# Last image's 3x3 convolution: nine taps per 8 rows, against four products of combined rows per 16 rows

## The chip, the cores and the metric

The kernel runs on one core of a Trainium2 chip. The metric is the device time of one execution in microseconds (us). TensorE (PE) does matrix products, VectorE (DVE), ScalarE (ACT) and GpSimd (POOL) work on elements, and SyncE (SP) issues the transfers.

## The reference, cut to what matters

Four images of 64 x 64 pixels and 96 channels pass four layers: a state-space layer with scans along rows and columns (layer 0), a separable convolution (layer 1), attention and a feed-forward net (layer 2), a Fourier filter and a feed-forward net (layer 3). Layer 1 is what is changed:

```python
y = jax.nn.relu(x)
y = lax.conv_general_dilated(y, dw_kernel, padding='SAME', feature_group_count=C)   # 3x3, per channel
y = y + dw_bias
y = lax.conv_general_dilated(y, pw_kernel, padding='SAME')                          # 1x1, 96 -> 96
y = y + pw_bias
inv = gamma * lax.rsqrt(moving_var + BN_EPS)
y = y * inv + (beta - moving_mean * inv)
...
t = t + attention(layernorm(t)); t = t + ffn2(layernorm(t))
t = t + filter(layernorm(t));    t = t + ffn3(layernorm(t))
```

All data are float32, but for the feed-forward nets, whose operands are rounded to fp8.

## The kernel before, in words

Channels lie on partitions, the 4096 pixels of an image along the free dimension, in 8 blocks of 512 (`BLK`, `NBLK`), each 8 rows of 64 (`RPB`, `HW`).

There are three parts in time. First a head: image 0's inputs for the scans. Then a long middle in which the scans of all four images run, in an order written out by hand (`tc.manual_schedule()`), while a planner (`pieces`, with credits per engine) puts the later layers of images 0 to 2 beside them. At last an end: `last_post` finishes layer 0 of image 3 (into `x1t`, the tile `side`, which stays in on-chip memory), beside the last of image 2's feed-forward net, and then `tail` calls `rest` for image 3. Head and end are outside the hand-written order: there, instructions of several generators are emitted in turn, and the order on an engine need not be that of emission.

`rest` is a list of stages. In its first, `layer1` does the convolution for one image. The constants merge depthwise and pointwise weights: `taps[:, ky * 3 + kx, :]` is the 1x1 matrix `pw` scaled per input channel by the 3x3 weight of that tap, so that both convolutions are one sum of nine 96 x 96 products. For a block of 8 rows, nine matmuls (L953) add up in one bank of PSUM (`p_l1`; the profile calls it `p_l`), each with a shifted window of the input:

```python
nc.tensor.matmul(
    p3[:, ra:rb, ca_:cb_], lhsT=taps[:, ky * 3 + kx, :],
    rhs=x[:, at + ra : at + rb, ca_ + dx : cb_ + dx], start=(k == 0), stop=(k == 8))
```

A tap that looks left or right leaves out a column, so it has 504 columns in place of 512; at the image's top and bottom a row is left out too. One ACTIVATE on ScalarE (L925) applies `l1s` (the scale and bias of the normalisation) and writes the block into `t`. VectorE does nothing for it.

What follows needs `t`: `layernorm(..., "t1", "ln_a")` begins with its first half of four blocks when `ready["t1"]` is 4, and its second half at 8. It takes the mean away by a matmul (`p_mean`, L997), copies the result on VectorE (L988), squares it on ScalarE (L989), sums the squares up by matmuls (`p_var`, L979), and scales (`p_rstd` L1049, DVE L1040). Then come attention (`p_tok`, `p_gram`, `p_att`), the feed-forward net, the filter and the last net.

The end uses eight banks of PSUM in turn (`bank_taker`), the first of which image 2's feed-forward net had last.

Image 0's convolution of layer 0 has a form of the kind that the change brings in: `convolve_pairs` in the head combines rows on VectorE (L448), multiplies (L463), and adds up on ScalarE and VectorE (L477 to L484).

Of the kernel before, what the change touches and what calls it, by code (L numbers as in the profile page):

```python
# [10 lines left out]
F32 = mybir.dt.float32  # L11
F16 = mybir.dt.float16
F8 = mybir.dt.float8e5
AF = mybir.ActivationFunctionType
ALU = mybir.AluOpType
# [4 lines left out]
HW = 64  # L20
L = HW * HW
C = 96
# [4 lines left out]
BLK = 512  # L27
NBLK = L // BLK
RPB = BLK // HW
# [4 lines left out]
def conv_taps():  # L34

    return [(1, 1)] + [(y, x) for y in range(3) for x in range(3) if (y, x) != (1, 1)]


def tap_window(ky, kx, r0):

    dy, dx = ky - 1, kx - 1
    ra, rb = max(0, -dy - r0), min(RPB, HW - dy - r0)
    ca, cb = max(0, -dx), min(HW, HW - dx)
    return dy, dx, ra, rb, ca, cb
# [4 lines left out]
NEXT = "next"  # L49
# [24 lines left out]
def layers(ctx: ExitStack, tc: tile.TileContext, a: dict, out):  # L74
# [4 lines left out]
    nc = tc.nc  # L79
# [11 lines left out]
    def dram(name, shape):  # L91
        return [dr.tile(shape, F32, tag=f"{name}{b}", name=f"{name}{b}") for b in range(NB)]
# [9 lines left out]
    x1 = dram("x1", [C, L])  # L102
# [20 lines left out]
    def steps_past(since, n):  # L123

        while ordered[0] and clock[0] < since + n:
            yield NEXT
# [8 lines left out]
    done = {}  # L135
# [44 lines left out]
    def rows_of(i):  # L180

        r0 = RPB * i
        return r0, max(r0 - 1, 0), min(r0 + RPB + 1, HW)
# [5 lines left out]
    def bank_taker(pool, n):  # L189

        free = [(pool, k) for k in range(n)]

        def take(name, rows=C, cols=BLK, held=()):
            while not free:
                yield NEXT
                if held:
                    yield from settle(held)
            bank = free.pop(0)
            t = bank[0].tile([128, BLK], F32, tag=f"bank{bank[1]}", name=name)

            def give(later=False):

                if later and ordered[0]:
                    returned.append((free, bank))
                else:
                    free.append(bank)

            return t[:rows, :cols], give

        return take, free  # L210

    def settle(held):


        while held:
            cost, f, args, since = held[0]
            if cost[1]:
                while ordered[0] and clock[0] == since and (clock[0] - 1) % 8 in (7, 0, 1):
                    yield NEXT
            yield cost  # L220
            held.pop(0)
            f(*args)

    def until(ready):
        while not ready():
            yield NEXT
# [641 lines left out]
    def blk(i):  # L868
        return slice(i * BLK, (i + 1) * BLK)
# [25 lines left out]
    def rest(b, take, deep, x1t=None, held=None):  # L895
# [3 lines left out]
        t = outer.sbuf(f"t{b}").tile([C, L], F32, tag="t", name="t")  # L899
        ready = {}  # L900
# [4 lines left out]
        def layer1(wk):  # L905
            x3 = (x1[b] if x1t is None else x1t).rearrange("p (r w) -> p r w", w=HW)

            def load(i):
                r0, lo, hi = rows_of(i)
                if x1t is not None:  # L910
                    return x3[:, lo:hi, :], clock[0]
                x = wk.tile([C, RPB + 2, HW], F32, tag="x", name="x", bufs=2)
                nc.sync.dma_start(x[:, : hi - lo, :], x3[:, lo:hi, :])
                return x, clock[0]

            def arrived(i):
                return done.get(("x1", b), 0) >= min(i + 2, NBLK)

            yield from until(lambda: arrived(0))
            nxt = load(0)  # L920
            yield NEXT
            held = []

            def finish(i, p, give):
                nc.scalar.activation(  # L925
                    t[:, blk(i)], p, AF.Identity, scale=l1s[:, 0:1], bias=l1s[:, 1:2]
                )
                give()
                ready["t1"] = i + 1

            for i in range(NBLK):
                r0, lo, hi = rows_of(i)
                if nxt is None:
                    yield NEXT
                    yield from settle(held)
                    yield from until(lambda: arrived(i))
                    nxt = load(i)
                    yield NEXT
                (x, since), nxt = nxt, None
                if clock[0] < since + LANDING:  # L940
                    yield NEXT
                    yield from settle(held)
                    yield from steps_past(since, LANDING)
                p, give = yield from take("p_l1", C, held=held)
                p3 = p.rearrange("p (r w) -> p r w", w=HW)
                for k, (ky, kx) in enumerate(conv_taps()):
                    if k % 3 == 0:
                        yield (2.4, 0, 0, 0, 0 if k else 1)
                        if nxt is None and i + 1 < NBLK and arrived(i + 1):
                            nxt = load(i + 1)  # L950
                    dy, dx, ra, rb, ca_, cb_ = tap_window(ky, kx, r0)
                    at = r0 + dy - lo
                    nc.tensor.matmul(  # L953
                        p3[:, ra:rb, ca_:cb_], lhsT=taps[:, ky * 3 + kx, :],
                        rhs=x[:, at + ra : at + rb, ca_ + dx : cb_ + dx],
                        start=(k == 0), stop=(k == 8),
                    )
                    if k == 2:
                        yield from settle(held)
                held.append(((0, 0.68, 0, 0), finish, (i, p, give), clock[0]))  # L960
            yield NEXT
            yield from settle(held)

        def layernorm(wk, hold, dst, source, result, previous=None):


# [451 lines left out]
        wk = normal.sbuf(f"ln{b}")  # L1418
# [3 lines left out]
        if deep > 1:  # L1422
# [4 lines left out]
        wk = mid.sbuf(f"mid{b}")  # L1427
        q8 = wk.tile([C, L], F8, tag="q8", name="q8")
        yield [
            *layernorm(wk, ln[:C, :], ln[:C, :], "t3", "ln_s", "q8"),  # L1430
            *feed_forward(wk, ffn2, q8, "q8", "t3"),
            *layernorm(wk, ln[:C, :], q8, "t2", "q8"),
            attention(wk, ln),
            *layernorm(wk, ln[:C, :], ln[:C, :], "t1", "ln_a"),
            layer1(wk),
        ], [mid] + ([held] if held else [])
        inner = Region(tc)
        yield filter_in(inner.sbuf(f"filter_in{b}"), ln), [inner, normal]
# [3 lines left out]
        vs = wide.sbuf(f"vs{b}").tile([128, N1, C], F32, tag="vs", name="vs")  # L1442
# [9 lines left out]
        wk = last.sbuf(f"last{b}")  # L1452
# [10 lines left out]
    def main_lane(take):  # L1463

        region = Region(tc)
        wk = region.sbuf("pre")
        images = [before_scans(b, wk, take, prev=b - 1 if b > 1 else None) for b in range(1, NB)]
        yield [chain(*parts) for parts in zip(*images)], [region, weights]
        done["pre"] = True
        for b in range(NB - 1):  # L1470
            yield from rest(b, take, 1)
# [33 lines left out]
    def tail(x1t, held):  # L1505

        region = Region(tc)
        take, _ = bank_taker(region.psum("tail_psum"), 8)
        yield from rest(NB - 1, take, 2, x1t, held)
        region.close()  # L1510
# [12 lines left out]
    def place_of(n, q):  # L1523


        return (4, 3, 2, 1)[q] if n % 2 else q
# [3 lines left out]
    while len(delta_places) <= N:  # L1530
        p = delta_places[-1]
# [204 lines left out]
    aside, weights, head, start = Region(tc), Region(tc), Region(tc), Region(tc)  # L1736
# [3 lines left out]
    wk = weights.sbuf("weights", side="right")  # L1740
    kept.append(const("gavg", [C, C], a["gavg"], wk))
    take, _ = bank_taker(start.psum("start_psum"), 2)
# [43 lines left out]
    wk = head.sbuf("pre0")  # L1786
    take, _ = bank_taker(head.psum("head_psum"), 8)
# [9 lines left out]
    take, banks = bank_taker(beside.psum("beside_psum"), 3)  # L1797
# [3 lines left out]
    with tc.manual_schedule():  # L1801
        ordered[0] = True
        pas = [decay(0, 0, True), None, None, None]
        for n in range(N + 1):
# [3 lines left out]
            for q in range(NCH):  # L1808
# [23 lines left out]
                s = Ss[n, q] = big.tile([128, CH], F32, tag=f"S{place_of(n, q)}", name="S")  # L1832
# [14 lines left out]
            if n % NG == 1 and n > 1:  # L1847
                b, o = halves[h - 1]
# [53 lines left out]
            if n % NG == NG - 4 and h + 1 < len(halves):  # L1902
                b, o = halves[h + 1]
# [7 lines left out]
    x1t = side[:, :L]  # L1911
# [125 lines left out]
```

## Time and profile before

| | us |
|---|---|
| median of the runs (5784.04, 5797.89, 5817.91) | 5797.89 |
| profiled execution: its own time | 5791.5 |
| profiled execution: span from first to last instruction | 5789.7 |
| image 3's layer 1 in it, first to last matmul start | 5412.3 to 5479.1 |

The page gives busy time by engine over the whole span: PE 72%, DVE 84%, ACT 52%, POOL 76%, and a mean granted TensorE clock of 0.771 of full speed. These are means over parts with different limits; what bears on the change is the stretch from 5388 to 5500 us. A float32 matmul of the program stands as two records in the trace (144 for the 72 of one image); below, one record is called a pass. The duration of a pass includes its latency; the pace is the distance from one start to the next.

### The profile page before, as it was taken

How to read it: one execution, taken by the hardware profiler on the slowest of the kernel's cores; microseconds unless marked ns; L12 is line 12 of the kernel's file. 1: busy time of each engine (PE TensorE's matmuls, PEld its weight loads, DVE VectorE, ACT ScalarE, POOL GpSimd, SP SyncE). 2: the span in 40 equal slices, each digit the busy share in tenths (PEclk: the TensorE clock that was granted, in tenths of full speed). 3: DMA queues.
4: the chain of work that ended last, by engine and by line, in shares of the span. 5: the costliest groups of instructions: out<-in, count | busy, mean ns of one | idle time of the engine just before them, and what ended most of it. 6: DMA issues, size and time to landing. Idle time of an engine off the chain costs nothing. (4 is left out here: it accounts for less than half of the span.)

```text
span 5789.7 us, 65093 instructions
## 1 busy us (share of the span) xinstructions
PE 4187.2 (72%) x19818; PEld 1630.1 (28%) x19818; DVE 4858.5 (84%) x3610; ACT 3020.1 (52%) x4188; POOL 4417.0 (76%) x2148
## 2 busy tenths in 40 slices
PE   8978887778864777664477776667778667667878
PEld 4422222222211221241331221334222114323345
DVE  4188988888899898999799999999999999978364
ACT  4767766766663356545454446444544544434233
POOL 1378887888898778888788989888898898867200
PEclk9888898888866876666777886678678666777888
DMA  4378878876699878788988868679887678886013
GB/s 123 111 212 229 233 200 235 233 204 196 195 252 236 225 206 222 207 240 244 255 235 224 228 182 222 197 210 248 235 235 202 171 207 237 251 227 183 20 43 101
DMA packets 470107, 1174.80 MB, mean 203 GB/s; under 512 B 90768, under 2 KB 155900, under 8 KB 469628
## 3 DMA queue, kind: packets, MB, share of 16 engines
q1 hardware_dynamic: 469756, 1170.64, 74.1%
q8 instruction: 157, 2.57, 0.2%
q14 instruction: 194, 1.59, 0.1%
HBM read 1013.53 MB, written 156.76 MB: 202 GB/s over the span
## 5 line engine op out<-in xcount | busy, mean ns | idle before, releaser
L1574 POOL TENSOR_TENSOR S<-S,rep 128x1024 f32<-128x1024 f32 x768 | 1807.2, 2356 | 546.2 <-DVE S L1894 495.1
L1587 ACT ACTIVATE pa<-dl,nega 128x1024 f32<-128x1024 f32 x1152 | 1285.3, 1117 | 1431.9 <-DVE S L1894 1072.3
L1570 POOL TENSOR_TENSOR B<-B,rep 128x1024 f32<-128x1024 f32 x768 | 1798.0, 2355 | 119.0 <-DMA B<-du_s 70.8
L1833 DVE TENSOR_TENSOR_SCAN S<-pa,S,B 128x1024 f32<-128x1024 f32 x576 | 1352.3, 2348 | 315.6 <-ACT pa L1587 133.5
L1601 PE MATMUL py<-S,red 128*32 128x512 f32 x3072 | 908.5, 848 | 755.1 <-POOL S L1574 503.6
L1884 DVE TENSOR_TENSOR_SCAN pa<-pa,edge,B 128x1024 f32<-128x1024 f32 x438 | 1029.7, 2351 | 55.5 <-ACT pa L1587 55.5
L1894 DVE TENSOR_TENSOR S<-S,pa 128x1024 f32<-128x1024 f32 x630 | 763.6, 1212 | 1.9
L1833 DVE TENSOR_TENSOR_SCAN S<-pa,B 128x1024 f32<-128x1024 f32 x192 | 436.4, 2273 | 44.8 <-ACT pa L1587 35.8
L1601 PEld LDWEIGHTS py<-S,red 128*32 128x32 f32 x3072 | 110.0, 125 | 1232.7 <-POOL S L1574 728.3
L402 PE MATMUL p_conv<-low,conv_w 128*96 128x512 f32 x864 | 437.4, 658 | 14.1 <-ACT u L414 9.6
L1884 DVE TENSOR_TENSOR_SCAN pa<-pa,B 128x1024 f32<-128x1024 f32 x192 | 440.8, 2296 | 5.3
L154 ACT COPY side<-side 96x256 f32<-96x256 f32 (+1 forms) x448 | 279.0, 629 | 187.7 <-DMA deltaT_s<-side 79.9
L1884 DVE TENSOR_TENSOR_SCAN dl<-pa,edge,B 128x1024 f32<-128x1024 f32 x138 | 323.1, 2341 | 20.6 <-ACT pa L1587 16.6
L1175 POOL CAST h<-y 128x1536 fp8e5<-128x1536 f16 x64 | 95.5, 1492 | 303.2 <-ACT y L886 281.9
L1579 POOL TENSOR_TENSOR dl<-dl,rep 128x1024 f32<-128x1024 f32 x138 | 325.6, 2360 | 0.1
L402 PE MATMUL p_conv<-high,conv_w 64*96 64x512 f32 (+1 forms) x576 | 269.7, 605 | 0.0
L997 PE MATMUL p_mean<-t,centre 96*96 96x512 f32 x256 | 173.7, 791 | 99.0 <-ACT sq L989 48.4
L402 PEld LDWEIGHTS p_conv<-low,conv_w 128*96 128x96 f32 x864 | 149.5, 181 | 319.0 <-issue 289.8
L1601 PE MATMUL py<-dl,red 128*32 128x512 f32 x552 | 220.2, 717 | 21.1 <-POOL dl L1579 21.1
L1609 ACT COPY ys<-py 128x512 f32<-128x512 f32 x384 | 221.8, 578 | 19.5 <-PE py L1601 18.3
L647 PE MATMUL p_y<-side,ident 96*96 96x512 f32 x336 | 210.0, 774 | 28.1 <-DVE side L681 8.6
L953 PE MATMUL p_l<-x,taps 96*96 96x504 f32 (+3 forms) x432 | 199.4, 613 | 16.2 <-DMA x<-x 12.7
(245 smaller groups left out, 6024.0 us busy)
## 6 DMA issues: line engine op xcount, KB each, us to landing
dl<-delta_s SPq DMA_DIRECT2D x768, 256.0 KB
B<-du_s SPq DMA_DIRECT2D x768, 256.0 KB
B<-duT_s SPq DMA_DIRECT2D x768, 256.0 KB
dl<-deltaT_s SPq DMA_DIRECT2D x768, 256.0 KB
z_s<-z SPq DMA_DIRECT2D x48, 512.0 KB
zl<-z_s SPq DMA_DIRECT2D x64, 384.0 KB
side<-y_s SPq DMA_DIRECT2D x120, 192.0 KB
rep<-bc_s SPq DMA_DIRECT2D x64, 256.0 KB
```

Source lines behind the costliest of these rows:

```text
L154: nc.scalar.copy(o.rearrange("p (w h) -> p w h", h=HW), t[:n, :].rearrange("p (h w) -> p w h", w=HW)[:, q * w : (q + 1) * w, :],)
L402: nc.tensor.matmul(p, lhsT=conv_w[: src.shape[0], k, oc * C : (oc + 1) * C], rhs=src[:, ky : ky + RPB, kx : kx + HW], start=(k == 0), stop ...
L647: nc.tensor.matmul(p, lhsT=ident[:C, :C], rhs=x, start=(j == 0), stop=(j == 2))
L1570: nc.gpsimd.tensor_tensor(Bs[n, q], Bs[n, q], reps[n // NG, 0, q], ALU.mult)
L1574: nc.gpsimd.tensor_tensor(Ss[n, q], Ss[n, q], reps[n // NG, 1, q], ALU.mult)
L1579: nc.gpsimd.tensor_tensor(dls[n, 0], dls[n, 0], reps[n // NG, 1, 0], ALU.mult)
L1587: nc.scalar.activation(pa, dls[n, q], AF.Exp, scale=nega[:, g : g + 1])
L1601: nc.tensor.matmul(py[32 * j : 32 * j + 32, :], lhsT=red, rhs=x[:, k * BLK : (k + 1) * BLK], start=(i == 0), stop=(i == len(terms) - 1),)
L1609: nc.scalar.copy(ys, pys.pop((n, half)))
L1833: nc.vector.tensor_tensor_scan(s, pas[q], Bs[n, q], Ss[n, q - 1][:, CH - 1 : CH] if q else 0.0, ALU.mult, ALU.add,)
L1884: nc.vector.tensor_tensor_scan(to[:, ::-1], pas[q][:, ::-1], Bs[n, q][:, ::-1], edge if k else 0.0, ALU.mult, ALU.add,)
L1894: nc.vector.tensor_tensor(Ss[n, q], Ss[n, q], to, ALU.add)
```

## The change

For image 3 alone, `layer1` is replaced by `layer1_pairs`. It takes 16 rows at a time as 8 pairs of an even and an odd row. Of the three kernel rows g0, g1, g2 (each three taps) it makes four combinations once: g0, (g0 + g1 + g2) / 2, (g0 - g1 + g2) / 2, g2. For each group it makes four combinations of input rows on VectorE, v0 to v3, with columns of zeros at both sides (set once by GpSimd, for two sets of buffers), multiplies each by its combination with three shifts along the row, and forms even and odd output rows from the four products. That is 4 x 3 matmuls of 512 columns for 16 rows, where `layer1` has 2 x 9.

```diff
+        def layer1_pairs(wk):
+            x3 = x1t.rearrange("p (j r w) -> p j r w", r=2, w=HW)
+            g = [taps[:, 3 * k : 3 * k + 3, :] for k in range(3)]
+            two = wk.tile([C, 2, 3, C], F32, tag="two", name="two")
+            plus, minus = two[:, 0], two[:, 1]
+            nc.vector.tensor_tensor(plus, g[0], g[2], ALU.add)
+            nc.vector.tensor_tensor(minus, plus, g[1], ALU.subtract)
+            nc.vector.tensor_tensor(plus, plus, g[1], ALU.add)
+            nc.vector.tensor_scalar(two, two, 0.5, None, ALU.mult)
+            g = [g[0], plus, minus, g[2]]
+            less = wk.tile([C, 1], F32, tag="less", name="less")
+            nc.vector.tensor_scalar(less, l1s[:, 0:1], -1.0, None, ALU.mult)
+            n = RPB
+            vs = [
+                [
+                    wk.tile([C, n, HW + 2], F32, tag=f"l1v{p}{k}", name="v") for k in range(4)
+                ]
+                for p in range(2)
+            ]
+            for v in (v for p in vs for v in p):
+                for col in (0, HW + 1):
+                    nc.gpsimd.memset(v[:, :, col : col + 1], 0.0)
+            for i in range(0, NBLK, 2):
+                j0 = i * RPB // 2
+                v0, v1, v2, v3 = (v[:, :, 1 : HW + 1] for v in vs[i // 2 % 2])
+                rows = x3[:, j0 : j0 + n]
+                d1, d2 = rows[:, :, 0, :], rows[:, :, 1, :]
+                yield from until(lambda: done.get(("x1", b), 0) >= min(i + 3, NBLK))
+                nc.vector.tensor_tensor(v1, d1, d2, ALU.add)
+                nc.vector.tensor_tensor(v2, d2, d1, ALU.subtract)
+                s = 1 if i == 0 else 0
+                if s:
+                    nc.vector.tensor_scalar(v0[:, 0], d2[:, 0], -1.0, None, ALU.mult)
+                nc.vector.tensor_tensor(
+                    v0[:, s:], x3[:, j0 + s - 1 : j0 + n - 1, 1, :], d2[:, s:], ALU.subtract
+                )
+                e = n - 1 if i == NBLK - 2 else n
+                if e < n:
+                    nc.vector.tensor_copy(v3[:, e], d1[:, e])
+                nc.vector.tensor_tensor(
+                    v3[:, :e], d1[:, :e], x3[:, j0 + 1 : j0 + e + 1, 0, :], ALU.subtract
+                )
+                out_rows = t[:, i * BLK : (i + 2) * BLK].rearrange(
+                    "p (j r w) -> p j r w", r=2, w=HW
+                )
+                even, odd = out_rows[:, :, 0, :], out_rows[:, :, 1, :]
+                for k in (1, 2, 0, 3):
+                    p, give = yield from take("p_l1")
+                    p = p.rearrange("p (j w) -> p j w", w=HW)
+                    for kx in range(3):
+                        nc.tensor.matmul(
+                            p, lhsT=g[k][:, kx, :], rhs=vs[i // 2 % 2][k][:, :, kx : kx + HW],
+                            start=(kx == 0), stop=(kx == 2),
+                        )
+                    if k == 1:
+                        nc.scalar.activation(
+                            odd, p, AF.Identity, scale=l1s[:, 0:1], bias=l1s[:, 1:2]
+                        )
+                    if k in (0, 2):
+                        nc.vector.scalar_tensor_tensor(
+                            even, p, l1s[:, 0:1], even if k == 0 else odd, ALU.mult, ALU.add
+                        )
+                    if k > 1:
+                        nc.vector.scalar_tensor_tensor(
+                            odd, p, less, odd, ALU.mult, ALU.add
+                        )
+                    give()
+                    yield NEXT
+                ready["t1"] = i + 2
...
-            layer1(wk),
+            layer1(wk) if x1t is None else layer1_pairs(wk),
```

Images 0 to 2 keep `layer1`.

## The prediction

> **What bounds the kernel now.** I read the busy times of the last 110 us in three windows first. Columns: stretch, its length, then busy us (instructions) of PE, its weight loads, DVE, ACT, POOL, the granted clock, the DMA share and GB/s.
>
> ```profile
> 5388.00:5412.30 24.30, 14.88 (x31) 4.54 (x29) 14.65 (x20) 11.14 (x18) 15.30 (x12) 0.57 0.12 34
> 5412.30:5479.60 67.30, 67.26 (x161) 25.70 (x162) 4.13 (x6) 11.17 (x16) 1.15 (x1) 0.97 0.02 6
> 5479.60:5500.00 20.40, 18.72 (x129) 10.69 (x127) 11.05 (x18) 7.90 (x14) 0.63 (x6) 1.00 0.00 1
> ```
>
> The middle one is image 3's convolution: PE is busy all of it at nearly full clock, DVE for 4 of 67 us. Next, the convolution's own row (minimum, median, maximum in ns, then first and last start) and the two longest idle times that belong to this stage in the list of waits:
>
> ```profile
> L953 PE MATMUL p_l<-side,taps x144: 533/586/1169, 5412.3 to 5479.1; 96*96 96x504 f32 x88, 96*96 96x512 f32 x44, 96*96 96x441 f32 x8, 96*96 96x448 f32 x4
> DVE ln L988 <- PE p_mean L997: 53.7, 8, 48.7
> ACT t L925 <- PE p_l L953: 53.4, 8, 8.8
> ```
>
> DVE and ACT wait for PE, and nothing else is under way: no DMA to speak of, POOL all but empty. All later layers of image 3 need `t`. So here **TensorE's passes are the time**, and a microsecond less of them ends the kernel a microsecond earlier, if nothing else comes in. The timeline shows how the stage starts and its pace (start, duration):
>
> ```profile
> 5411.60 0.69 DVE L881 CAST z<-p_f 96x512 f16<-96x512 f32 x1 [1.46 <-PE p_f L1186]
> ...
> 5412.34 47.72 PE L953 MATMUL p_l<-side,taps 96*96 96x512 f32 x108 [0.85 <-DVE z L881]
> ...
> 5429.51 0.77 ACT L925 ACTIVATE t<-p_l,l1s 96x512 f32<-96x512 f32 x1 [6.87 <-PE p_l L953]
> ...
> 5437.16 0.77 ACT L925 ACTIVATE t<-p_l,l1s 96x512 f32<-96x512 f32 x1 [6.87 <-PE p_l L953]
> ```
>
> It begins when image 2's last `z` has left the PSUM bank that `p_l1` takes first. A block of 18 passes takes 5437.16 - 5429.51 = 7.65 us: 0.425 us per pass.
>
> **What the Trainium skill says.** "TensorE: Matmul & The Clock Gate", Part 1, has the array at half clock after an idle window of some 3.4 us, and at full after a busy one. The trace agrees: in the first 4.7 us of the stage the granted clock is 0.58 and two passes stand 0.85 us apart, then 0.425. "VectorE: DVE Perf Modes", the perf-mode tier table, says that a float32 tensor_tensor produces one result per cycle, however its operands lie; at its 0.96 GHz, 512 results are 0.53 us. The trace agrees: 0.68 us for one, 0.60 from start to start. "SBUF — State Buffer", Who interferes with whom, says that DVE with two SBUF inputs is in the way of a GpSimd instruction that reads SBUF. L739 agrees (median and maximum are 0.69 and 1.74 us, the latter beside POOL's adds).
>
> **The change, part by part.**
>
> *Passes removed.* 144 go. At 0.425 us that is 61.2; the two edge blocks leave out 64 or 63 columns in six passes each, 760 columns, 0.6 us. So 60.6. *Passes added:* 4 groups x 4 products x 3 shifts x 2 = 96, all of 512 columns. Their pace is that of `p_mean`, also 512 columns: weight loads at 5513.24 and 5513.67, 0.43 apart. 96 x 0.428 = 41.1. Saved on the path: **19.5 us**. The start at half clock (some 1.6 us) and the 3.4 us of `p_mean` and 1 us of `p_var` in the stage stay.
>
> *Start.* Four operations on 96 x 288 elements combine weights (four of 264 elements take 1.46 us in the head, L448), then v1, 0.7: 2.2 us before the first product can start. They need only `taps` and `x1t` (whole by 5389), so they can run before 5412, as other work of image 3 does:
>
> ```profile
> 5396.62 3.51 POOL L1425 MEMSET turned<- 1x4096 f32 x1
> ...
> 5396.72 3.56 DVE L890 TENSOR_SCALAR z<-z,b_L 96x512 f16<-96x512 f16 x1
> ```
>
> This memset is image 3's, and lies inside image 2's net (and makes a 0.35 us operation of DVE last 3.56). Then they cost slots of DVE, 14.65 of 24.3 us busy, in front of image 2's `z`. Between 0 (in gaps) and 4 us (behind `z`, or in front of it beside POOL's reads); I take 1.5. The 16 memsets of edge columns go through POOL's queue (128 x 4 elements take 0.10 us, L1083), 1.6 us, before image 2's casts to fp8 or after: 0 to 2, I take 0.5.
>
> *Rows combined.* 16 operations of 512 elements at 0.60 are 9.6 us of DVE; two small ones at the edges 0.4. *Sums.* 12 SCALAR_TENSOR_TENSOR from PSUM in place of 8 ACTIVATEs of ACT, of which 4 stay:
>
> ```profile
> L1129 DVE SCALAR_TENSOR_TENSOR t<-p_att,at_bias,t x8: 746/746/747, 5505.5 to 5513.0; 96x512 f32<-96x512 f32 x8
> ```
>
> 12 x 0.75 = 9 us. With layernorm's first half (4 copies, 2 for the rate, 4 scalings, 6.5 us) DVE has 25 us of work in a stage of some 47 us: PE covers it. If that cover goes, the cost is the exposed chain. Within a group, a product takes 6 x 0.428 = 2.57 us, DVE needs 0.6 for a row combination and at most 1.5 for sums: no stall. Between groups, were v1 of the next queued behind the last sum, PE would wait 0.75 + 0.6 and some 0.2 of signals, three times, 4.7 us. In the head the same form of work does not go that way:
>
> ```profile
> 206.62 0.41 DVE L483 TENSOR_TENSOR u<-u,p_conv 96x256 f32<-96x256 f32 x1
> 207.47 0.43 DVE L448 TENSOR_TENSOR v<-low 128x264 f32<-128x264 f32 x1 [0.44 <-ACT low L347]
> 207.82 0.41 DVE L484 TENSOR_TENSOR u<-u,p_conv 96x256 f32<-96x256 f32 x1
> ```
>
> The next block's combination stands before the sum of the one in hand. With two sets of buffers I expect this here too, and take 1.0 of 0 to 5. New waits: DVE waits for products in four banks per group; behind it stand the next v and layernorm's copies, for which PE waits only when all eight banks are full.
>
> *End.* Blocks 6 and 7 are complete together. The four `p_mean` begin with blocks 4 and 5, 1.7 us, which cover the last sum (0.75 + 0.2): 0 to 1, I take 0.3.
>
> *Later stages.* Nothing is edited, but their order may shift: -2 to 2, I take 0. No transfer is moved or added; image 3's input is already on chip.
>
> **Sum:** -19.5 + 1.5 + 0.5 + 1.0 + 0.3 = -16.2 us, with bounds of -21.5 and -5.5. On the profiled execution's 5791.5 (span 5789.7 and 1.8 around it) that is 5775.3. The median shown is 6.4 higher, and -16.2 on it gives 5781.7. I forecast **5780**.
>
> **The rivals.**
>
> *The clock falls in part.* If PE idles a little at each product it may lose clock, not only time: from 5500 to 5550 PE is busy for 43.5 of 50 us and is granted 0.69. At a mean of 0.8, 41.1 becomes 51.4 and the gain 6: **5792**. For it: DVE now stands between every two products. Against: twice as much PE time as DVE time, eight banks.
>
> *The slower end: half clock throughout.* If DVE's turn leaves PE idle for so large a part of the stage that the clock stays as from 5388 to 5412 (61% busy, 0.57), each pass takes 0.853: 81.9 for the products in place of 60.6, 4.4 more for `p_mean` and `p_var`, 3.3 as above: +29, **5827**. It decides between 87% and 61% of PE busy. Against: DVE has 25 us of work in this time.
>
> *The gain is given back.* Either fewer passes aren't what the program issues (the row's count would stay 144; the code's loops give 96), or the order of the later stages, 310 us with their own waits, changes by as much as is saved: **5798**. Against: PE's chain after the convolution has one thread and the edit doesn't touch it.
>
> *More gain.* The convolution overlaps image 2's net, as products in banks that are free earlier go first: some 10 us more, **5770**. Against: the first product takes the late bank, and PE keeps its order.
>
> **How the numbers follow.** A change under 0.5% (29 us) is about what a measurement of this kernel can't tell from none; the runs shown span 34 us. My forecast 0.68, clock in part 0.13, slower end 0.05, given back 0.09, more gain 0.05. Even the whole saving, 19.5 us, is 0.34%: only scatter makes that faster by over 0.5%. Faster 0.08 (scatter on forecast and more gain), slower 0.07 (the slower end and some scatter), within 0.85. Range: the forecast's bounds on the median are 5776 to 5792; with the two middle rivals and half the runs' scatter it is 5764 to 5802.
>
> **What would show it.** Right: a row of `p_l` with 96 passes, all of 512 columns, at a 0.43 pace; some 47 us from its first pass to the last, PE busy above 95% and clock at 0.95; DVE some 25 us busy there; the start within 3 us of 5412; the same 310 us after it. Wrong: passes at 0.85; PE waiting for `v` or for a bank between products; a start beyond 5416 with image 2's `z` delayed by memsets or combinations; or a convolution shorter by 19 us and an end that isn't.

## The result, and the profile after

The changed kernel takes 5788.66 us (median of 20 runs, 5776.59 to 5793.85); the kernel before, run beside it, 5798.73 (20 runs, 5784.04 to 5821.08). The ratio is 0.9979, with a 95% interval of 0.9970 to 0.9988: 12 us less, between 7 and 17 (the two medians differ by 10). The forecast was 5780 in a range of 5764 to 5802. The profiled execution of after took 5793.85 us, its span is 5792.0. In it the last scan, which both kernels share, ends 6.3 us later than in the profile of before (5347.9 in place of 5341.6), so below lengths of stages are compared, not times on the clock.

First the busy times of three stretches of after: the wait ahead of the first product, the convolution, and what follows up to the last `p_gram`. Columns: stretch, length, busy us (instructions) of PE, its weight loads, DVE, ACT, POOL, then granted clock, DMA share, GB/s.

```profile
5420.90:5425.00 4.10, 0.02 (x1) 0.05 (x1) 4.10 (x9) 0.72 (x1) 1.85 (x19) 0.50 0.31 90
5425.00:5474.20 49.20, 49.20 (x113) 17.89 (x113) 22.93 (x36) 8.13 (x12) 0.00 (x0) 0.93 0.00 0
5474.20:5501.50 27.30, 21.29 (x129) 13.39 (x128) 11.88 (x19) 7.00 (x12) 0.63 (x6) 0.81 0.00 1
```

The middle line is what was wanted: PE is busy for all of 49.20 us at a clock of 0.93, and DVE, with 22.93 us of work, never holds it up. The lines on either side have no like in the kernel before. In the first, PE stands still while DVE is busy to the last hundredth. In the last PE is busy for 21.29 of 27.30 us at 0.81; before, the stretch from 5479.6 had 20.4 us, 18.72 busy, at 1.00.

The convolution's row and two waits of after, to be laid beside those of before:

```profile
L1019 PE MATMUL p_l<-v,taps x48: 592/592/1139, 5425.0 to 5473.7; 96*96 96x512 f32 x48
L1019 PE MATMUL p_l<-v,two x48: 592/592/1061, 5426.8 to 5468.5; 96*96 96x512 f32 x48
```

```profile
PE p_l L1019 <- DVE v L1002: 4.9, 1, 4.9
...
PE p_rstd L1124 <- DVE rs_y L1104: 4.4, 1, 4.4
```

There are 96 passes in place of 144, all of 512 columns. And there are two waits of PE, each once: 4.9 us ahead of the first product, for a row combination, and 4.4 us after the last, for the rate of layernorm.

**The start**, in the timeline of DVE and then of PE (start, duration):

```profile
5420.19 0.69 DVE L881 CAST z<-p_f 96x512 f16<-96x512 f32 x1 [1.46 <-PE p_f L1261]
5420.80 0.44 DVE L973 TENSOR_TENSOR two<-taps 96x288 f32<-96x288 f32 x1
5421.16 0.14 DVE L979 TENSOR_SCALAR less<-l1s 96x1 f32<-96x1 f32 x1
5421.23 0.68 DVE L997 TENSOR_TENSOR v<-side 96x512 f32<-96x512 f32 x1
5421.82 1.40 DVE L974 TENSOR_TENSOR two<-two,taps 96x288 f32<-96x288 f32 x1
5423.15 0.68 DVE L998 TENSOR_TENSOR v<-side 96x512 f32<-96x512 f32 x1
5423.75 0.44 DVE L975 TENSOR_TENSOR two<-two,taps 96x288 f32<-96x288 f32 x1
5424.12 0.18 DVE L1001 TENSOR_SCALAR v<-side 96x64 f32<-96x64 f32 x1
5424.22 0.61 DVE L1002 TENSOR_TENSOR v<-side 96x448 f32<-96x448 f32 x1
```

```profile
5424.98 1.99 PE L1019 MATMUL p_l<-v,taps 96*96 96x512 f32 x2 [4.90 <-DVE v L1002]
5426.77 7.71 PE L1019 MATMUL p_l<-v,two 96*96 96x512 f32 x12
```

Every combination that the first group needs stands behind image 2's last `z`, though their inputs were whole before. One of 288 elements (L974) takes 1.40 us where its like take 0.44: POOL's addition L1271, 5421.71 to 5422.91, lies beside it. The first pass on PE has `v0`, the third that DVE makes (the loop names `v1` first; its weights `two` are whole only after `v0`). From the start of that cast to the first pass it is 4.79 us, where it was 0.74 before.

**After the last product**, PE's timeline:

```profile
5474.20 1.11 PE L1124 MATMUL p_rstd<-rs_y,pick 32*96 32x512 f32 x8
5476.07 1.66 PE L1153 MATMUL p_tok<-ident,ln 96*128 96x96 f32 x11 [0.76 <-DVE ln L1115]
...
5479.49 0.85 PE L1141 MATMUL p_gram<-lt 128*97 128x97 f32 x8
5480.18 3.60 PE L1072 MATMUL p_mean<-t,centre 96*96 96x512 f32 x8
5483.71 1.66 PE L1054 MATMUL p_var<-sq,mean_w 96*32 96x512 f32 x6
...
5486.15 1.04 PE L1054 MATMUL p_var<-sq,mean_w 96*32 96x512 f32 x2
5491.60 2.04 PE L1124 MATMUL p_rstd<-rs_y,pick 32*96 32x512 f32 x8 [4.40 <-DVE rs_y L1104]
5494.36 2.02 PE L1153 MATMUL p_tok<-ident,ln 96*128 96x96 f32 x11 [0.72 <-DVE ln L1115]
```

And the same place in the kernel before:

```profile
5479.46 3.60 PE L997 MATMUL p_mean<-t,centre 96*96 96x512 f32 x8
5482.99 1.66 PE L979 MATMUL p_var<-sq,mean_w 96*32 96x512 f32 x6
5484.58 1.09 PE L1049 MATMUL p_rstd<-rs_y,pick 32*96 32x512 f32 x2
5485.61 1.04 PE L979 MATMUL p_var<-sq,mean_w 96*32 96x512 f32 x2
5486.58 1.11 PE L1049 MATMUL p_rstd<-rs_y,pick 32*96 32x512 f32 x6
5487.62 0.55 PE L1078 MATMUL p_tok<-ident,ln 96*128 96x96 f32 x4
```

These two lists are the main finding. The same passes stand in another order. Before, the second half's `p_mean` and `p_var` come straight after the convolution, and the first half's `p_rstd`, `p_tok` and `p_gram` after them: they fill PE while ACT and DVE work out the second half's rate. After, the first half goes first (6 us, 5474.20 to 5480.18), and when the rate is awaited nothing is left: PE idles for 4.40 us and then goes on at half clock, eight `p_rstd` in 2.04 us in place of 1.11.

### The profile page after: what moved, and what is told of

It reads as the page before. It is cut to its first block, busy times and chain, and to the rows that moved or that the text cites. A ratio compares the mean times of both kernels' runs of the same rounds, so it can differ in the third digit from the quotient of the medians.

```text
span 5792.0 us, 65076 instructions
## 1 busy us (share of the span) xinstructions
PE 4191.9 (72%) x19770; PEld 1625.2 (28%) x19770; DVE 4882.4 (84%) x3649; ACT 3015.3 (52%) x4184; POOL 4418.5 (76%) x2164
```

## The experiments

The time of a whole run scatters by more than these steps: the end of the scans lies between 5333.7 and 5360.4 us in the profiles below, and differs by 3 to 13 us between two profiles of one kernel. So each kernel has its stages read from its profile, between marks that all share. A is the first `p_f2` pass (the profile calls it `p_f`) after image 2's last `p_rstd`, B the start of image 2's last group of `p_f2`, C the first product of image 3's convolution, D the end of its last one, E the end of the last `p_gram`. The last two columns are the difference of A to E from before, and the time against before: ratio, interval, and the difference in us that the ratio makes on the median of before in those runs.

| kernel | A-B | B-C | C-D | D-E | A-E | A-E less before | time |
|---|---|---|---|---|---|---|---|
| before | 20.67 | 2.29 | 67.29 | 20.05 | 110.30 | | |
| after | 20.59 | 6.34 | 49.29 | 27.22 | 103.44 | -6.9 | 0.9979 (0.9970-0.9988), -12 |
| after_again | 20.67 | 6.34 | 49.32 | 27.23 | 103.56 | -6.7 | 0.9983 (0.9972-0.9994), -10 |
| order_kept | 20.65 | 6.34 | 49.30 | 20.13 | 96.42 | -13.9 | 0.9976 (0.9965-0.9987), -14 |
| weights_early | 25.21 | 2.29 | 48.99 | 27.12 | 103.61 | -6.7 | 0.9991 (0.9981-1.0001), -5 |
| order_and_weights | 25.21 | 2.29 | 49.06 | 20.06 | 96.62 | -13.7 | 0.9981 (0.9970-0.9993), -11 |
| products_alone | 20.73 | 2.28 | 48.02 | 26.56 | 97.59 | -12.7 | 0.9973 (0.9963-0.9984), -16 |
| nine_taps_by_turns | 20.70 | 2.29 | 75.04 | 20.34 | 118.37 | +8.1 | 1.0018 (1.0006-1.0030), +10 |
| no_turns | 20.58 | 6.34 | 44.61 | 28.88 | 100.41 | -9.9 | 0.9960 (0.9945-0.9975), -23 |
| no_turns_again | 20.58 | 6.33 | 44.60 | 28.88 | 100.39 | -9.9 | 0.9961 (0.9941-0.9981), -23 |
| weights_from_head | 25.22 | 2.29 | 49.02 | 20.05 | 96.58 | -13.7 | 0.9965 (0.9951-0.9978), -20 |
| combined_after_cast | 20.53 | 4.64 | 48.36 | 20.12 | 93.65 | -16.7 | 0.9978 (0.9968-0.9987), -13 |
| two_buffers_by_vector | 20.75 | 2.94 | 48.08 | 20.12 | 91.89 | -18.4 | 0.9947 (0.9927-0.9968), -31 |

Where nothing was touched, a stage comes out within some 0.2 us (A-B in ten profiles: 20.53 to 20.75). The times cannot tell steps of 4 us apart. The part behind E, which no edit touches, is 290.0 us in before, 290.5 and 290.3 in the two profiles of after, and 287.0 to 292.1 over all. (The expectations give the start of the stretch as the end of the last scan; A is nearer and carries none of that scatter.)

Theory ahead of the experiments: after gives back 4 us at the start, because DVE makes the combinations late, and 7 us after the convolution, because `layer1_pairs` yields after each product and so lets the first half of what follows be issued ahead of the second half. Rivals: the loss after the convolution is the clock, or DVE's sums; the loss at the start is GpSimd's memsets.

**order_kept.** After, with no turn in the last group:

```diff
-                    yield NEXT
+                    if i < 6:
+                        yield NEXT
```

Expected:

> The changed kernel, but the generator hands on its turn after a product only in the first three groups, no more in the last; the second half's means then stand directly behind the last product on TensorE, as in the kernel before. Order theory: from the end of the last product to the end of p_gram it takes 20 to 21 us (27.3 in the changed kernel, 20.1 in the kernel before), and the whole is some 17 us under the kernel before in place of 10. Clock theory (the 27.3 us come from a clock that happened to be half after a pause, not from the order): 25 us or more remain, and the whole stays some 10 us under. Start theory says nothing of this one: the first product still starts some 4.8 us after the start of image 2's last z.

Measured: D-E is 20.13 in place of 27.22, all else as in after. Its timeline of PE shows the order of before again:

```profile
5460.57 5.31 PE L1019 MATMUL p_l<-v,taps 96*96 96x512 f32 x12
5465.72 3.60 PE L1073 MATMUL p_mean<-t,centre 96*96 96x512 f32 x8
5469.25 1.66 PE L1055 MATMUL p_var<-sq,mean_w 96*32 96x512 f32 x6
5470.84 1.09 PE L1125 MATMUL p_rstd<-rs_y,pick 32*96 32x512 f32 x2
```

The order is the cause; sums and combinations are unchanged here, so the rival of DVE falls, and that of the clock too, by which 25 us or more would have remained. In time it gained only some 2 us on after, within the intervals: 14 us under before, where 17 were expected. The stages do not say why. Its sixteen `p_att` passes start at half clock and take 9.74 us (before: 9.58), and those of after 7.11 in both profiles; but the whole part behind E is 287.5 us in order_kept, 3 us shorter than in after.

**nine_taps_by_turns** is the counter-test: the kernel before, its nine taps untouched, with turns after each block of image 3 (`settle` issues ScalarE's write of that block at once):

```diff
                 held.append(((0, 0.68, 0, 0), finish, (i, p, give), clock[0]))
+                if x1t is not None:
+                    yield from settle(held)
+                    yield NEXT
+                    yield NEXT
+                    yield NEXT
+                    yield NEXT
```

> The kernel before, with its nine taps and ScalarE's write, but the convolution of image 3 hands on its turn after each block (four times in a row), as the changed kernel does after each product. Order theory: emission by turns alone makes the second half's means stand behind the first half's attention work or leaves the second half's rate chain uncovered; from the end of the last product to the end of p_gram there are pauses of TensorE of 5 us or more which the kernel before hasn't, and from the start of image 2's last product to the end of p_gram it is 4 to 8 us more than the kernel before's 89.6. Rival (the loss in the changed kernel comes from its products or from VectorE's sums): 89.6 within 1.5.

A-E is 8.1 us longer than before, and the time is 10 us longer, with an interval that lies above 1. The loss is at the upper end of the 4 to 8 us expected; the pause, 4.39 us, is shorter than the 5 expected. In the timeline of PE the same hole as in after, without one product of combined rows:

```profile
5488.33 1.05 PE L985 MATMUL p_var<-sq,mean_w 96*32 96x512 f32 x2
5493.77 2.04 PE L1055 MATMUL p_rstd<-rs_y,pick 32*96 32x512 f32 x8 [4.39 <-DVE rs_y L1035]
```

Here the first half's `p_rstd`, `p_tok` and `p_gram` (5.9 us from 5453.82) lie ahead of the convolution's last 54 passes. That work has moved from D-E into C-D, and in D-E the pause has taken its place: so the table shows the loss in C-D.

**no_turns** and **no_turns_again**: after with no `yield NEXT` in the loop at all.

> The changed kernel, its generator never handing on its turn within the convolution. All 48 products then stand in front of both halves' means. Order theory: the second half's means come at once, but the first half's rate chain (some 4 us) is no longer under the products: the time from the last product to the end of p_gram lies between 20 us plus the 4.4 us of the first half's means and sums that moved behind, and 29; the products' own stretch gets 4.4 us shorter, so that from the first product to the end of p_gram it is 70 to 73 (76.5 in the changed kernel, 69.4 with the turn kept in three groups).

> no_turns once more, as its time (23 us under before) was the lowest although its stretch from the end of the scans to the last p_gram, 148.7 us, is longer than that of order_kept (145.7) and combined_after_cast (142.8). If the stages decide and the rest is scatter of the scan part, the stretch is 147 to 150 again and the time 12 to 19 under before; if something outside this stretch favours it, 20 to 26 under before again.

PE does all 48 matmuls in one piece (44.6 us), then all eight blocks' means and variances, and waits once, for the first half's rate; the second half's is covered.

```profile
5455.92 7.03 PE L1071 MATMUL p_mean<-t,centre 96*96 96x512 f32 x16
5462.88 2.52 PE L1053 MATMUL p_var<-sq,mean_w 96*32 96x512 f32 x16
5469.94 2.03 PE L1123 MATMUL p_rstd<-rs_y,pick 32*96 32x512 f32 x8 [4.54 <-DVE rs_y L1103]
```

First product to last `p_gram` is 73.5 us, just above the 70 to 73 expected, and 4 us more than with order_kept. Yet both times are 23 us under before, 13 us more than A to E explains. Of the two expectations for the second run, the one of the stages holds for the trace (the stretch is 149.5 us) and the other for the time. In both profiles the part behind E is 287.0 us, 3 us shorter than in before; the other 10 us are in no stage that was compared, and stay open.

**products_alone** has no row combinations, no combined weights and no sums: products read the rows of layer 0's result as they are, and ACT writes both outputs. Layer 1's result is another one.

```diff
-                            p, lhsT=g[k][:, kx, :], rhs=vs[i // 2 % 2][k][:, :, kx : kx + HW],
+                            p, lhsT=g[k][:, kx, :], rhs=rows[:, :, k % 2, :],
```

> The changed kernel without VectorE's part: no weight or row combinations, no sums, no memsets; the same 96 passes of 512 columns read the image's rows as they are, and ScalarE writes even and odd rows from two of the four products (the result of layer 1 is thus another one). It shows what TensorE's passes alone are worth. If VectorE costs only the start, the first product starts 0.7 us after the start of image 2's last z, first to last product takes 47 us (49.2 in the changed kernel), the stretch after it stays at 27 us since the order is the same, and the whole is some 15 us under the kernel before. If VectorE also holds up products in the middle (rival), the passes here are closer together than 0.43 us apart from pauses in the changed kernel, and more than 6 us are saved over it.

C-D is 48.02, against 49.29 with all of DVE's work. The 1.3 us lie at the start: in after the weight loads are 0.85 us apart from 5425.9 to 5431.0, and 0.43 from 5431.7 on. So DVE's 23 us inside the convolution cost nothing; the 4 us of its work ahead of it cost 4 us of waiting (B-C 6.34 against 2.28), and the start at half clock is longer by what costs 1.3 us. D-E stays at 26.56: the turns are still there.

**weights_early** makes the combined weights (L973 to L979) at the head of `last_post`, in spare columns of `side`:

```diff
+        two = spare[:, : 6 * C].rearrange("p (a k c) -> p a k c", a=2, k=3)
+        nc.vector.tensor_tensor(two[:, 0], g[0], g[2], ALU.add)
...
```

> The changed kernel, but the weight combinations are made earlier, beside the last part of layer 0 of image 3, in spare columns of the tile side; row combinations stay. Start theory (VectorE's queue of weights and rows delays the first product): the first product starts 1.5 to 2 us after the start of image 2's last z in place of 4.8, the half-clock stretch at the start is no longer than in the changed kernel, and the whole is 13 us under the kernel before. Rival (the wait is for something else than the weights, such as the columns of zeros from GpSimd, set 2.7 to 3.3 us after that start): the first product still starts after 3.5 us or more. Order theory: the stretch from the last product to the end of p_gram stays at 27 us.

The first product waits only for `z` again, B-C falls by 4.05 us (6.34 to 2.29), and A-B grows by 4.6 (20.59 to 25.21): nothing is won. **order_and_weights** has this and the edit of order_kept:

> Both edits together. Order and start theories: 20 us under the kernel before (5779 where that has 5799), the two savings of 7 and 3 us on top of the 10. If the time after the convolution is set by the clock and not by order, 13.

It repeats both effects (A-B 25.21, D-E 20.06), and the 20 us expected do not come: it is 11. **weights_from_head** tests whether the five weight operations themselves delay image 2: there the head makes them, they wait in HBM, and one load brings them to `side` in `last_post`; turns are as in order_kept.

> The changed kernel with the turn handed on in the first three groups alone, and with the weight combinations made in the head, kept in HBM, and loaded by one transfer of 222 KB into spare columns of the tile side in the end. Start and order theories: the first product starts 2.3 us after image 2's last product starts (6.3 in the changed kernel), and the stretch between the last scan and that product stays at 69 to 71.5 us, as no operation of VectorE is added there (73.5 to 74.8 when the combinations were made there). From the last scan's end to the end of p_gram some 141 us, against 153.6 in the changed kernel and 158.1 in the kernel before; the whole 18 to 20 us under the kernel before. Rival: the transfer or its place in SP's queue delays the loads of y_in, and the stretch before grows by 2 us or more.

A-B is 25.22 again: the weights were not it. DVE's timeline in this kernel shows what is:

```profile
5394.48 3.29 DVE L901 TENSOR_SCALAR y<-y,b_L 128x512 f16<-128x512 f16 x1 [0.22 <-ACT y L890]
5397.69 0.67 DVE L1005 TENSOR_TENSOR v<-side 96x512 f32<-96x512 f32 x1
5398.28 0.68 DVE L894 CAST y<-p_f 128x512 f16<-128x512 f32 x1
...
5403.41 0.68 DVE L1004 TENSOR_TENSOR v<-side 96x512 f32<-96x512 f32 x1
5404.01 1.95 DVE L1005 TENSOR_TENSOR v<-side 96x512 f32<-96x512 f32 x1
5405.88 0.68 DVE L1009 TENSOR_TENSOR v<-side 96x512 f32<-96x512 f32 x1
5406.48 0.68 DVE L1015 TENSOR_TENSOR v<-side 96x512 f32<-96x512 f32 x1
5407.09 0.68 DVE L894 CAST y<-p_f 128x512 f16<-128x512 f32 x1
```

With the weights out of the workspace, the row buffers `v` lie at other addresses, free earlier, and nine row combinations move ahead of image 2's last casts; so far this is argued, and the next run tests it. PE waits for those casts: 4.33 and 3.19 us at once, in this kernel's timeline of PE.

```profile
5399.01 0.59 PE L1249 MATMUL p_f<-q,w_L 96*128 96x512 fp8e5 x1 [4.33 <-DVE y L894]
...
5407.81 0.58 PE L1249 MATMUL p_f<-q,w_L 96*128 96x512 fp8e5 x1 [3.19 <-DVE y L894]
```

Not all of the first wait is row combinations: the operation of 3.29 us (L901) lies beside GpSimd's memset of `turned` (5394.11 to 5397.62), which here comes ahead of a cast to fp8 that it follows in the kernel before. The second set of buffers lets even the second group's combinations go ahead of image 2's end, where they are of no use yet.

**combined_after_cast** puts the buffers back: weights_from_head, with a hole in the workspace where the weights were.

```diff
+            wk.tile([C, 2, 3, C], F32, tag="two", name="two")
+            wk.tile([C, 1], F32, tag="less", name="less")
             n = RPB
             vs = [
```

> weights_from_head with one difference: the workspace keeps a hole of the size of the weight combinations, so that the row buffers v lie where they lie in the changed kernel, in memory that image 2's net gives up last. Then VectorE's first row combination stands directly behind image 2's last z cast, and the first product is one with v1. In weights_from_head nine row combinations stood in front of that cast, and the stretch from the end of the scans to image 2's last p_f2 group was 73.6 us, against 68.4 before and 70.7 after. Theory (row combinations ahead of the cast delay image 2's end by as much as they bring the first product forward): that stretch is 68 to 71 again, the first product starts 2.9 to 3.2 us after the last p_f2 group (2.3 in weights_from_head, 6.3 after), the stretch from the end of the scans to the last p_gram is 140 to 143 (144.9 in weights_from_head, 158.1 before), and the time is 20 to 26 us under before. Rival (the stretch is longer for another reason, the load of the weights or the clock): it stays at 73 or more, and the time is that of weights_from_head or 1 us above.

A-B is 20.53 again, so the place of the buffers was the cause. The load is still there, so the rival of the transfer falls. With the row combinations that memset of GpSimd is back in its old place too (behind the cast, at 5409.47), and the run does not tell the shares of the two apart. The first product, though, begins 4.64 us after B, not 2.9 to 3.2. POOL's timeline, then PE's:

```profile
5425.97 1.38 POOL L1281 TENSOR_TENSOR t<-t,z 96x512 f32<-96x512 f32 x1 [1.75 <-ACT z L899]
5427.29 0.63 POOL L998 MEMSET v<- 96x8 f32 x16
```

```profile
5427.54 2.02 PE L1028 MATMUL p_l<-v,side 96*96 96x512 f32 x2 [3.20 <-POOL v L998]
```

The memsets, cheap as they are (0.63 us for 16), stand in POOL's queue behind an addition that waits for the same `z`. In after they were hidden by DVE's longer queue. **two_buffers_by_vector** has DVE set the columns of the first two buffers:

```diff
+            for v in (vs[0][1], vs[0][2]):
+                for col in (0, HW + 1):
+                    nc.vector.memset(v[:, :, col : col + 1], 0.0)
```

> combined_after_cast with one difference: the four columns of zeros of the first two buffers used (v1 and v2 of the first set) are set by VectorE, directly behind image 2's last z cast, in place of GpSimd, where all 16 stood behind the residual add that waits for the same cast. Theory (there the first product waited for GpSimd's memsets, 5427.3 to 5427.9, and not for VectorE, whose v1 was whole at 5425.7): the first product starts 3.1 to 3.5 us after image 2's last p_f2 group (4.64 in combined_after_cast, 6.34 after), all other stages as in combined_after_cast (68 to 71 from the end of the scans to that group, 48 to 48.5 from first to last product, 20.1 to the last p_gram). Rival (the start is set by something else that comes with the cast): 4.6 again. The time is 12 to 24 us under before either way; what is at stake, 1.3 us, shows in the trace alone.

B-C is 2.94, slightly less than expected, A-E 91.9, the shortest of all: 18.4 us less than before, and 11.5 less than after. Its ratio is the lowest as well, 5776.57 us against 5800.94, but from 6 runs, and 31 us is more than the stages show. Its interval lies below 1 and below those of after and after_again, each taken against the kernel before in other runs, so it is faster than before and most likely than after; that it is worth all of 31 us is not claimed.

**after_again:**

> The changed kernel once more, for a second profile and a second comparison. If the stages hold: first to last product 49.3 us, first product 6.3 us after image 2's last p_f2 group, 27.2 from the last product to the last p_gram, 10 to 14 us under before. If the loss of 7 us after the convolution or of 4 us ahead of it belonged to the one execution that was profiled, they are not there.

Both losses are there again within 0.01 us: they belong to the program, not to one execution.

## Why the prediction was right, and where its sum was not

The direction and the size came out: 16.2 us less was forecast, 12 (7 to 17) measured. The size is in part luck, as the stages show less than half of the forecast. The terms, from the table, before to after:

- *Passes.* Forecast -19.5, found -18.0 (67.29 to 49.29). 96 passes at 0.43, as said. Most of the 1.5 us missing is half clock: that the start at half clock, "some 1.6 us", stays was wrong in size: it cost 2.0 us in before and 3.4 in after.
- *Start.* Forecast +2.0 (1.5 for DVE and 0.5 for the memsets), found +4.05 (2.29 to 6.34). The case that came, "behind `z`", was priced at 4. The 2.2 us that the forecast had for weights and `v1` became 4.05: by the timeline above the weights took 2.1, 1.0 of them beside POOL's addition, and `v1`, `v2` and `v0` 1.9. One of its signs of being wrong, a start beyond 5416, came true: less the 6.3 us of the scans, the start is at 5418.7. The term was mis-sized by taking a value between two cases that exclude each other: the row combinations are either ahead of `z` (then A-B pays 4.5 to 4.6 us, as weights_early and weights_from_head show) or behind it (then B-C does). The cheap middle, all combinations in DVE's gaps, did not occur in any kernel. The memsets cost nothing in after, and 1.7 us where DVE no longer hid them (4.64 less 2.94).
- *Stalls between groups.* Forecast +1.0, found none. The next group's row combinations do stand ahead of the sums in hand, as in the head.
- *End and later stages.* Forecast +0.3 and 0, found +7.2 (20.05 to 27.22). **This is the step that failed.** "The four `p_mean` begin with blocks 4 and 5" took for granted that they follow the last product, and "PE's chain after the convolution has one thread and the edit doesn't touch it" was wrong: the two halves of layernorm are two threads, and a `yield` in the new loop decides which is issued first. The wait for the rate was in the kernel before as well, under cover. It was the cover that moved.

In total -18.0 + 4.05 + 7.2 makes -6.8 in the two profiles; from the last `p_gram` to the end they differ by 0.5 us (290.0 and 290.5), although `p_att` gained 2.5. The comparison of times says 7 to 17, at whose lower end the stages lie. That the forecast came so near to the 12 measured is luck: a failure of 7 us lies inside the scatter of the runs. The rival "the gain is given back", which named the order of the later stages, had the mechanism, and some 60% of the saved passes were indeed given back in the trace (11.2 of 18.0). That a change under 0.5% can't be told from none was too cautious: with 20 runs of each kernel, 0.21% has an interval clear of 1.

The clock's rivals fell: 0.93 in the convolution. What "stays" at its start is not of one size. From the first weight load to the first at full pace it is 4.0 us in before and in nine_taps_by_turns, 4.2 in products_alone, 4.3 in two_buffers_by_vector, 5.0 in combined_after_cast, 6.0 to 6.1 in the three kernels with combinations ahead of `z`, and 6.7 to 6.8 in the five profiles that start as after does; half of each is lost. The Trainium skill ("TensorE: Matmul & The Clock Gate", Part 1) says that the array goes to full clock after a busy window of some 3.4 us, and that these windows run freely, whatever the program does; a start would then take between one and two of them, 3.4 to 6.8 us by an estimate from that page. The values lie in it, and in each trace's record of the clock all changes lie on one grid of 3.41 us. But kernels with the same stretch ahead of the start agree within 0.1 us, as do two profiles of one kernel, where freely running windows would let them differ; what ties them is not shown. After the convolution, too, the page fits: PE was at full clock ahead of the wait of 4.40 us and at half after it, and a wait of 0.76 us in before left it at full.

What stays open: why no_turns and two_buffers_by_vector are faster by 12 to 13 us more than A to E says. The part behind E accounts for 3 us in no_turns (287.0 against 290.0) and for none in two_buffers_by_vector (290.1). Only 6 to 11 runs stand behind each of these times.

## What to carry to other kernels

When a stage is rewritten, ask of the stage behind it what covers its longest wait, and whether the new loop gives its turn away at the same points as the old one: here the order of issue, not the work, took 7 of 18 us. Work that is moved ahead on a full queue is not free because it is ready early; it must stand behind whatever the other engines wait for, and if it cannot be in a gap, its cost only changes places. And a short chain that is hidden by a longer one (the memsets) becomes the limit as soon as the longer one is cut.

## What the runs showed of the hardware

- Small DVE operations on on-chip data that ran beside POOL's addition lasted until its end or a little longer: 288 elements took 1.40 us in place of 0.44 (L974 of after). In combined_after_cast an operation on 64 elements took 1.14 us, where the same one took 0.18 in after, and the addition lay from 5425.97 to 5427.35:

```profile
5426.26 1.14 DVE L1010 TENSOR_SCALAR v<-side 96x64 f32<-96x64 f32 x1
```

- The Trainium skill ("SBUF — State Buffer", Who interferes with whom) has it that DVE and GpSimd share a pair of ports which one of them locks, that a DVE operation with two inputs in SBUF (the on-chip memory) contends for it with a GpSimd operation that reads there, and that the order of issue decides who waits. The trace agrees: the combination that DVE had begun at 5425.66, before that addition, took its usual 0.68 us, and the addition 1.38 in place of 1.15.
- The start at half clock ahead of the same stage cost 2.0 us in one kernel and 3.4 in another. A gain of 1 us at such a place is not to be promised.
